# Three projections of five token blocks as seven products of half-size matrices

## The chip, the cores and the metric

The kernel runs on one core of a Trainium2 chip. TensorE (PE) multiplies matrices, with a queue of its own for loading weights (PEld); VectorE (DVE), ScalarE (ACT) and GpSimd (POOL) work on tiles; SyncE (SP) issues almost all DMAs. PE writes to eight PSUM banks of 128 x 512 F32; DVE and ACT read them[...]. The metric is the device time of one execution in microseconds (us), lower is better.

## The reference

The input x has 4 sequences of 1024 tokens with 512 features, so 4096 rows. The first part below is `_L0_attn_ref`, the second `_L0_ffn_ref` (512 to 1536 to 512 features, its weights rounded to fp8), the last two lines join them; their weight arguments are left out:

```python
lam = _decay_lambda(beta)
q = (x @ Wq.T).reshape(Bsz, Ls, NHEAD, HEAD_DIM)
v = (x @ Wv.T).reshape(Bsz, Ls, NHEAD, HEAD_DIM)
ret = _retention_scan(v, lam)              # state = lam * state + v_t
out = (q * ret).reshape(Bsz, Ls, D)
out = _layernorm(out, ln_gamma, ln_beta)
g = jax.nn.silu(x @ Wg.T)
out = out * g
return out @ Wo.T
...
gate = jax.nn.silu(_quantized_matmul(x, gate_w, gate_scale))
up = _quantized_matmul(x, up_w, up_scale)
fuse = gate * up
return _quantized_matmul(fuse, down_w, down_scale)
...
x = x + _layernorm(_L0_attn_ref(_layernorm(x, axis=-1)), axis=-1)
x = x + _layernorm(_L0_ffn_ref(_layernorm(x, axis=-1)), axis=-1)
```

## The kernel before

The 4096 tokens are cut into eight blocks of 512 (NB = 8, TB = 512), the 512 features into four chunks of 128 (NC = 4), the 1536 inner features of the FFN into twelve (NI = 12). One class, `Retention`, does a block's attention half, `Ffn` its FFN half. The main loop runs over the FFN's blocks, t = 0 to 7, and in each over twelve steps i. At a given t three blocks are in work: `a` (block t) is in its FFN, `b` (block t+1) in its attention, `n` (block t+2) is loaded, normalised and transposed, and `l` (block t-1) gets its last layernorm, residual and store.

A step i of the FFN has three parts on PE: `f.gate(i)` and `f.up(i)`, 8 matmuls each in F32R (the activations are kept as an upper part and a remainder, both F32R), and `f.down(i - 2)`, 8 more. Between these parts the loop puts the attention work. For the projections, `project` (line 282) does one chunk of 128 output features for 512 tokens: 4 F32 matmuls of 128 x 512 that add up in one PSUM bank. `v(c)` and `q(c)` run in steps 11 (c = 0, block n), 0, 1 and 2; `scan(c)` runs the recurrence on DVE straight from PSUM, and `y_of(c)` multiplies q by it. Step 3 has chunk 0 of g and the mean over features (`mean`: a matmul of the sum over chunks, split by `halves` into an upper part on ACT and a remainder on DVE, with a matrix of 1/512); `center_y` subtracts it on DVE, squares on ACT and adds the squares on POOL. Step 4 has chunk 1 of g, `var` and `rstd_y` (a root on ACT and a reciprocal on DVE), steps 5 and 6 the rest of g and `z(c)`, which scales and gates chunk c of y. Steps 7 to 10 have the output projection `o(s)` for four groups of 128 tokens, and the moments and sums that follow it; step 11 ends with the transposes of the fourth group.

Order: every engine runs its instructions in the order in which the program issues them (class `InOrder`); the order in the loop is written out by hand. A wait of one instruction therefore holds everything behind it on its engine. The same holds for SP: a DMA that waits for its data keeps the later DMAs back.

PSUM: `ps_a` has two banks that v, q, g, mean, var and o use in turn (name "pa"), `ps_f` two for gate and up (the transposes of step 11 use one of them too), `ps_d` four for the sums of `down`. `halves` and the squares share one scratch tag of two tiles ("ret"), x1n, the FFN's results d and other tiles of 128 x 512 one of four ("tok").

The weights wv_sb, wq_sb and wg_sb (1 MB each) stay in SBUF for the whole run. The input of the projections, xnT, lies as [128 features, 16 groups, 4 chunks, 32 tokens], as it comes out of 32 x 32 transposes by DVE and a trip through DRAM (`send_x`, `fetch_x`); `by_chunk` is its view by chunk, whose runs are 32 tokens long.

Normalising on DVE with two scalars per token row (`center_scale`) serves x of blocks 3 to 7 (`norm_x`) and the FFN's results (`norm`). POOL computes 1/sqrt by a power (`rstd_in_place`).

Of the kernel before, what the change touches and what calls it, by code (L numbers as in the profile page):

```python
# [17 lines left out]
P = 128  # L18
# [5 lines left out]
def retention_ffn_sandwich(  # L24
# [36 lines left out]
    dram = ctx.enter_context(tc.tile_pool(name="dram", bufs=2 * NS, space=bass.MemoryType.DRAM))  # L61
    ps_a = ctx.enter_context(tc.tile_pool(name="ps_a", bufs=2, space=bass.MemoryType.PSUM))
    ps_f = ctx.enter_context(tc.tile_pool(name="ps_f", bufs=2, space=bass.MemoryType.PSUM))
# [228 lines left out]

    homes = {"pa": ps_a, "pf": ps_f, "pd0": ps_d, "pd1": ps_d, "pd2": ps_d, "pd3": ps_d}

    def ps_tile(name, home="pa"):
        return homes[home].tile([P, TB], F32, tag=home, name=name)

    def turn(src, name, home="pa"):
        pt = homes[home].tile([P, NC, P], F32, tag=home, name=name)
        for c in range(NC):  # L300
            pe.transpose(pt[:, c, :], src[:, ts(c, P)], ident)
        return pt

    def turn_by_blocks(dst, src, tag, name):
# [10 lines left out]
        sp.dma_start(dst, m)  # L315

    class Retention:


        def __init__(self, t, xt=None):  # L320
            self.t = t
            self.xt = xt or [load_x(t, s, [sp]) for s in range(NS)]
            self.mv = small.tile([P, NS, 2], F32, tag="mv4", name=f"mv4_{t}", bufs=2)
            self.pv, self.pq, self.pg, self.ret, self.g = {}, {}, {}, {}, {}
            self.po, self.mvo, self.x1n, self.ptx, self.kept = {}, {}, {}, {}, {}
            self.center = shift_scale if t < 2 else center_scale


# [58 lines left out]


        def v(self, c, home="pa", tokens=slice(None)):
            if c not in self.pv:  # L390
                self.pv[c] = ps_tile(f"pv_{self.t}_{c}", home)
            project(self.pv[c], wv_sb, c, [self.by_chunk], tokens)
# [49 lines left out]
        def mean(self):  # L442
            self.mu = ps_tile(f"mu_{self.t}")
            self.average(self.mu)
# [14 lines left out]
        def var(self):  # L459
            var = ps_tile(f"var_{self.t}")  # L460
            self.average(var)
            self.sum = work.tile([P, TB], F32, tag="rstd", name=f"rstd_{self.t}", bufs=1)
            act.activation(self.sum, var, AF.Sqrt, bias=eps_sb)
# [17 lines left out]

        def z(self, c):

            y = self.y
            dve.scalar_tensor_tensor(
                y[:, c, :], y[:, c, :], gamma_sb[:, c : c + 1], self.sum, ALU.mult, ALU.mult
            )
            dve.scalar_tensor_tensor(
                y[:, c, :], y[:, c, :], lnb_sb[:, c : c + 1], self.g.pop(c), ALU.add, ALU.mult
            )  # L490

# [57 lines left out]
    class Ffn:  # L549
# [68 lines left out]
        def rstd(self, s=None):  # L618
            if s is None:
                rstd_in_place(self.mv[:, :, 1], NS)  # L620
            else:
                rstd_in_place(self.mv[:, s, 1:2], 1)

        def rstd_by_root(self, s):
# [181 lines left out]
    for t in range(NB):  # L806
        f, n = Ffn(a), None
        for i in range(NI):
            if t > 0 and (t > 1 or i):
# [10 lines left out]
            if l and not b and i == 3:  # L820
                for s in range(NS // 2, NS):
                    l.scale(s)
            if l and b and i == 3:
                l.norm(0)
                l.add(0)
                l.norm(1)
                l.add(1)
            if l and not b and i in (6, 7):
                for s in range(2 * i - 12, 2 * i - 10):
                    l.norm(s)  # L830
                    l.add(s)
            if n and i == 6 and t > 0:
                n.stats(2)
                n.stats(3)
                n.rstd()
            if b and i == 5:
                b.z(0)
# [6 lines left out]
            for _ in range(look[i] // 2 if t == 1 else 0):  # L844
                next(search)

            if b and t == 0 and i < 2:
                b.q(i + 2, tokens=slice(None) if i else later)
                b.y_of(i + 2)
            if b and t > 0 and i < 3:  # L850
                b.v(i + 1)
                b.scan(i + 1)
            if l and b and i == 2:
                l.stats(0)
                l.stats(1)
            if b and i == 3:
                b.halves()
                units()
                if t == 0:
                    rounds(3, now=False)  # L860
                b.g_of(0)
                b.mean()
                b.center_y()
                if t == 0:
                    n.stats(3)
                    n.rstd()
                    n.shift()
            if b and i == 4:
                b.halves()
                if t == 0:  # L870
                    rounds(3, now=False)
                b.g_of(1)
                b.var()
            if b and i == 5:
                b.g_of(2)
                b.z(1)
            if b and i == 6:
                b.g_of(3)
                b.z(2)
                if t == 0:  # L880
                    b.z(3)
# [10 lines left out]
            if b and 7 <= i <= 10:  # L892
                b.o_moments(i - 7)
            units()
            f.up(i)
            f.fuse(i)
            if b and i == 4:
                b.rstd_y()
            if n and i == 11:
                n.v(0)  # L900
                n.scan(0)
                b.turn_x1n(3, "pf")
                b.upper_of(3)
            if t == 0:
                if i < 8 and i != 3:
                    rounds(3, now=False)
                f.rest(i)
                if i < 3:
                    n.stats(i)
            for _ in range((look[i] + 1) // 2 if t == 1 else 0):  # L910
                next(search)

            if l and b and i == 2:
                l.stats(2)
                l.stats(3)
                l.rstd()
            if l and not b and i in (4, 5):
                l.stats(2 * i - 8)
                l.stats(2 * i - 7)
                if i == 5:  # L920
                    l.rstd()
            if l and b and i == 3:
                l.norm(2)
                l.add(2)
                l.norm(3)
                l.add(3)
            if b and t > 0 and i < 3:
                b.q(i + 1)
                b.y_of(i + 1)
            if b and i == 6 and t > 0:  # L930
                b.z(3)
            if n and i == 5 and t > 0:
                n.stats(0)
                n.stats(1)
# [6 lines left out]
            if n and t > 0 and 6 <= i <= 9:  # L941
                n.norm_x(i - 6)
                n.send_x(i - 6)
# [7 lines left out]
            if n and i == 11:  # L951
                n.q(0)
                n.y_of(0)

# [6 lines left out]
            if b and not n and i == 11:  # L961
                b.turn_x1n(3)
                b.upper_of(3)
                b.rest_of(3)
                f.down(NI - 2)
            if b and i == 4 and 0 < t < NB - 2:
                n = Retention(t + 2)
# [75 lines left out]
```

## Time and profile before

| what | value |
|---|---|
| device time, three runs | 1005.61 to 1007.07 us, median 1006.77 |
| profiled execution | 1006.49 us; its span, first to last instruction, 1004.7 us |
| granted TensorE clock | 0.998 of full |
| DMA | 73.79 MB, mean 73 GB/s |
| a block in the steady part (t = 4) | 121.8 us |
| steps 0 to 2 of it, each | 12.33 us |
| steps 3 and 4, each | 9.34 us |
| steps 5 to 10, each | 8.89 us |
| step 11 | 12.78 us |

The costliest groups of instructions (matmul and weight load apart; in the group view the duration of a matmul is a modelled one, longer than the distance to the next, so the distance between starts is what PE pays):

| group | count | busy us |
|---|---|---|
| up, gate, down matmuls (F32R) | 768, 768, 768 | 215.3, 190.3, about 201 |
| v, q, g, o matmuls (F32, two records each) | 280, 272, 256, 256 | 115.0, 115.3, 114.8, 114.5 |
| DVE remainder of fuse | 90 | 79.4 |
| DVE product of gate and up | 96 | 71.7 |
| ACT SiLU of the gate | 96 | 65.9 |
| POOL x + x1n | 32 | 49.1 |

A row of the time view is: start, duration, engine, line, operation, output and inputs, shapes, count, and in brackets the idle time before it and what ended it. All engine calls go through one helper, so nearly every row says L74; one reads by tile names. pv, pq, pg, mu, var and po are the PSUM tiles of v, q, g, mean, variance and output projection.

### The profile page before, as it was taken

The numbers are of one execution on the slowest core, as the hardware profiler recorded it, in microseconds if no ns is written. First come the engines' busy times: TensorE is split into PE (matmuls) and PEld (weight loads), VectorE is DVE, ScalarE is ACT, GpSimd is POOL, SyncE is SP. The second block draws the span as 40 slices with busy tenths as digits, with TensorE's granted clock in tenths as the row PEclk, the third lists the DMA queues.
The fourth block names the chain that finished last, engine by engine and source line by source line (L and its number), as shares of the span: only waits on it lengthen the run. The fifth ranks groups of instructions, "written<-read, shape, count | busy, mean of one in ns | idle before, by whom it ended". The sixth has DMA issues, their size and how long they took to land.

```text
span 1004.7 us, 9838 instructions
## 1 busy us (share of the span) xinstructions
PE 988.9 (98%) x3518; PEld 653.6 (65%) x3518; DVE 633.8 (63%) x949; ACT 330.1 (33%) x494; POOL 234.8 (23%) x282
## 2 busy tenths in 40 slices
PE   8999999999999999999999999999999999999996
PEld 6456756666666666666666666666666656767885
DVE  5996977527766376753767547674576726746445
ACT  3546574434664133111322114211141111412223
POOL 1405112214122140311413114131132302213020
PEclk9999999999999999999999999999999999999999
DMA  9312314400125004350103402052021510004021
GB/s 296 113 63 91 119 43 105 126 1 22 63 84 147 0 33 146 94 126 1 69 26 108 112 1 84 19 134 79 1 84 37 132 63 11 32 24 123 1 84 42
DMA packets 62608, 73.79 MB, mean 73 GB/s; under 512 B 5856, under 2 KB 36320, under 8 KB 62560
## 3 DMA queue, kind: packets, MB, share of 16 engines
q1 hardware_dynamic: 60976, 72.24, 23.8%
q10 hardware_dynamic: 1584, 0.94, 0.4%
q8 instruction: 27, 0.44, 0.2%
q14 instruction: 21, 0.17, 0.1%
HBM read 43.53 MB, written 29.62 MB: 73 GB/s over the span
## 4 chain that ended last, share of the span: by engine, by line
PE 90%; DVE 4%; DMA 2%; ACT 1%; POOL 1%; issue 1%; SPq 0%; DVEq 0%; POOLq 0%
PE pfu L74 16%; PE pfg L74 16%; PE pd L74 16%; PE pv L74 11%; PE pg L74 10%; PE pq L74 10%; PE po L74 9%; DMA xnT<-mx 1%; DVE scr L74 1%; DMA mx<-xn 1%; DVE st L74 1%; POOL x L74 1%; DVE d L74 1%; DVE xn L74 0%; DMA beta_sb<-in_beta 0%
## 5 line engine op out<-in xcount | busy, mean ns | idle before, releaser
L74 PE MATMUL pfu<-x1nT,up_sb 128*128 128x512 f32 x768 | 215.3, 422 | 0.0
L74 PE MATMUL pfg<-x1nT,gate_sb 128*128 128x512 f32 x768 | 190.3, 390 | 0.4 <-DVE x1nT L74 0.4
L74 PE MATMUL pd<-down_sb,fuse 128*128 128x512 f32 x720 | 188.4, 403 | 0.0
L74 PEld LDWEIGHTS pfu<-x1nT,up_sb 128*128 128x128 f32 x768 | 144.5, 188 | 55.3 <-issue 28.2
L74 PEld LDWEIGHTS pfg<-x1nT,gate_sb 128*128 128x128 f32 x768 | 144.0, 188 | 30.6 <-DVE x1nT L74 0.8
L74 PEld LDWEIGHTS pd<-down_sb,fuse 128*128 128x128 f32 x720 | 135.2, 188 | 38.0 <-issue 10.8
L74 ACT CAST fuse<-gate 128x512 fp32r<-128x512 f32 x90 | 55.7, 618 | 269.0 <-DVE gate L74 269.0
L74 ACT ACTIVATE gate<-pfg,gs_sb 128x512 f32<-128x512 f32 x96 | 65.9, 686 | 221.9 <-PE pfg L74 221.8
L74 DVE SCALAR_TENSOR_TENSOR gate<-pfu,us_sb,gate 128x512 f32<-128x512 f32 x96 | 71.7, 747 | 98.6 <-PE pfu L74 98.4
L74 PE MATMUL pv<-xnT,wv_sb 128*128 128x512 f32 (+1 forms) x280 | 115.0, 557 | 4.0 <-ACT xnT L74 2.7
L74 PE MATMUL pq<-xnT,wq_sb 128*128 128x512 f32 (+1 forms) x272 | 115.3, 567 | 0.0
L74 PE MATMUL pg<-xnT,wg_sb 128*128 128x512 f32 x256 | 114.8, 592 | 0.0
L74 PE MATMUL po<-wo_sb,y 128*128 128x512 f32 x256 | 114.5, 592 | 0.0
L74 POOL TENSOR_SCALAR mv<-mv 128x1 f32<-128x1 f32 (+1 forms) x77 | 18.2, 237 | 314.3 <-DVE mv L74 313.7
L74 PEld LDWEIGHTS pv<-xnT,wv_sb 128*128 128x128 f32 x280 | 52.6, 189 | 52.3 <-issue 45.7
L74 DVE TENSOR_TENSOR fuse<-gate,fuse 128x512 fp32r<-128x512 f32 x90 | 79.4, 883 | 9.7 <-ACT fuse L74 9.7
L74 PEld LDWEIGHTS pq<-xnT,wq_sb 128*128 128x128 f32 x272 | 50.8, 190 | 46.8 <-issue 44.5
L74 PEld LDWEIGHTS po<-wo_sb,y 128*128 128x128 f32 x256 | 48.4, 189 | 50.1 <-issue 47.9
L74 PEld LDWEIGHTS pg<-xnT,wg_sb 128*128 128x128 f32 x256 | 48.4, 189 | 50.1 <-issue 47.2
L74 POOL TENSOR_TENSOR x<-x,x1n 128x512 f32<-128x512 f32 x32 | 49.1, 1533 | 44.4 <-DVE x1n L74 35.5
L74 DVE TENSOR_TENSOR_SCAN ret<-lam,pv 128x512 f32<-128x512 f32 x16 | 19.5, 1219 | 55.4 <-PE pv L74 55.4
L74 DVE BATCH_NORM_STATS2 st<-x 128x6 f32<-128x512 f32 x64 | 43.6, 681 | 14.0 <-POOL x L74 11.2
(114 smaller groups left out, 918.3 us busy)
## 6 DMA issues: line engine op xcount, KB each, us to landing
kept<-x SPq DMA_DIRECT2D x32, 256.0 KB, 2.1
x<-kept SPq DMA_DIRECT2D x32, 256.0 KB, 4.1
x<-in_x SPq DMA_DIRECT2D x28, 256.0 KB, 3.8
out<-d SPq DMA_DIRECT2D x27, 256.0 KB, 2.0
xnT<-mx SPq DMA_DIRECT2D x24, 256.0 KB, 4.7
mxs<-xs SPq DMA_DIRECT2D x84, 64.0 KB, 1.8
x1n<-mxs SPq DMA_DIRECT2D x21, 256.0 KB, 2.7
mx<-xn SPq DMA_DIRECT2D x20, 256.0 KB, 2.3
```

The source lines that it names most:

```text
L74: return lambda *args, **kwargs: tc.keep_in_program_order(op(*args, **kwargs))
```

## The change

For blocks 3 to 7 (`FAST = 3`) the three projections are computed by Strassen's scheme. The weight (512 x 512) and the input (512 x 512 tokens) are cut into halves both ways, and seven products of 256 x 256 by 256 x 256 take the place of eight: four matmuls of 128 x 256 for each product. The precision of the matmuls stays F32.

- `weight_sums` forms four sums of weight quarters for each projection on DVE in steps 0 and 1 of t = 1, and stores them in DRAM (twelve tiles of 256 KB). The resident weights are given up after step 6 of t = 1; their space becomes `t_sums` (four sums of input quarters), `w_ring` (four slots for weight operands) and `mids` (four tiles of 128 x 512 for intermediate results).
- `fetch_weights` loads the operand of a later product from DRAM into the ring: each product, once issued, orders the operand of the fourth product after it, into its own slot.
- `input_sums` forms the four input sums on POOL, at step 11.
- `product` issues the matmuls of the next product. Products that have a term in common add up in the same bank of PSUM; in between, DVE adds banks to `mids`. `take` uses a finished quarter of the result: a scan of half length for v, a product with y for q, a SiLU for g.
- The order is moved: at step 11 `input_sums(1, 2)` before up, two products after up, one and `input_sums(3, 4)` before down, one after down; at steps 0, 1 and 2 a product each after gate, up and down; then two at step 3, three at 4, two at 5, one at 6. The mean is now issued at the end of step 3, the variance at the end of step 4; all scaling of y by gamma is in step 5, all gating in step 6.
- The FFN's results d and x of these blocks are normalised by ACT (`norm_shifted`, `norm_x(.., True)`), with shift and scale made on POOL; the last two additions of d move from step 3 to step 4; statistics of x move to the end of step 5.
- The two "pa" banks get names of their own, pa0 and pa1, so that a product can ask for one.

```diff
@@ banks
-    ps_a = ctx.enter_context(tc.tile_pool(name="ps_a", bufs=2, space=bass.MemoryType.PSUM))
+    ps_a = ctx.enter_context(tc.tile_pool(name="ps_a", bufs=1, space=bass.MemoryType.PSUM))
@@ new, before class Retention
+    FAST = 3
+    H = TB // 2
+    order = [("v", j) for j in (1, 6, 2, 7, 4, 5, 3)]
+    order += [("q", j) for j in (1, 6, 2, 7, 4, 5, 3)]
+    order += [("g", j) for j in (1, 2, 6, 7, 4, 5, 3)]
+    banks = {"v": {1: 0, 6: 1, 5: 0}, "q": {1: 1, 6: 0, 5: 1}, "g": {1: 0, 6: 0, 5: 1}}
...
+    def weight_sums():
+        for k, (src, w) in squares.items():
...
+            for j, x, y, op in (
+                (5, a21, a22, ALU.add), (6, 5, a11, ALU.subtract),
+                (7, a11, a21, ALU.subtract), (3, a12, 6, ALU.subtract),
+            ):
+                t = work.tile([P, D], F32, tag="tok", name=f"sum_{k}{j}", bufs=4)
...
+                dve.tensor_tensor(done[j], x, y, op)
...
+                sp.dma_start(operands[k][j], done[j])
+                yield
...
+    def fetch_weights():
+        n = fetched[0]
+        if n < total_products:
+            k, j = order[n % len(order)]
+            sp.dma_start(w_ring[:, n % RING], operands[k][j])
+            fetched[0] += 1
@@ class Retention
+        def input_sums(self, *which):
+            x = self.by_chunk
+            b11, b12, b21, b22 = (
+                x[:, i : i + 2, g : g + TB // Q // 2, :] for i in (0, 2) for g in (0, TB // Q // 2)
+            )
+            ts_ = [t_sums[:, k].rearrange("p c (g j) -> p c g j", j=Q) for k in range(4)]
+            self.right = {1: b11, 2: b21, 3: b22, 5: ts_[0], 6: ts_[1], 7: ts_[2], 4: ts_[3]}
+            ops = {1: (ts_[0], b12, b11), 2: (ts_[1], b22, ts_[0]), 3: (ts_[2], b22, b12), 4: (ts_[3], b21, ts_[1])}
+            for k in which:
+                dst, x, y = ops[k]
+                pool.tensor_tensor(dst, x, y, ALU.subtract)
...
+        def product(self):
+            k, j = order[self.made]
+            n = (self.t - FAST) * len(order) + self.made
+            self.made += 1
+            w = w_ring[:, n % RING]
+            if j in (1, 6, 5):
+                bank = ps_tile(f"p{k}{j}_{self.t}", f"pa{banks[k][j]}").rearrange("p (c f) -> p c f", c=2)
...
+            bank = self.bank_b if j in (6, 7, 4) else self.bank_a
+            for o in range(2):
...
+                for c in range(2):
+                    pe.matmul(
+                        out_, w[:, c, ts(o, P)], self.right[j][:, c],
+                        start=(j in (1, 6, 5) and o == 0 and c == 0), stop=True,
+                        skip_group_check=True,
+                    )
+            fetch_weights()
+            c12, p1, s167 = (mids[:, m] for m in (1, 2, 3))
+            if j == 1:
+                act.copy(p1, bank)
+            elif j == 6:
+                dve.tensor_tensor(c12, bank, p1, ALU.add)
+            elif j == 7:
+                dve.tensor_tensor(s167, bank, p1, ALU.add)
+            elif j == 2:
+                self.take(k, 0, 0, bank)
+            elif j == 4:
+                dve.tensor_tensor(p1, bank, p1, ALU.add)
+                self.take(k, 1, 0, p1)
+            elif j == 5:
+                dve.tensor_tensor(s167, bank, s167, ALU.add)
+                self.take(k, 1, 1, s167)
+            else:
+                dve.tensor_tensor(c12, bank, c12, ALU.add)
+                self.take(k, 0, 1, c12)
@@ main loop
+            if fast and i in (0, 1, 2, 3, 4, 5, 6):
+                b.product()
...
+            if n and n.fast and i == 11:
+                n.input_sums(1, 2)
...
+                if n.fast:
+                    n.products(2)
...
+            if fast and i < 6:
+                b.product()
...
+                if n.fast:
+                    n.product()
+                    n.input_sums(3, 4)
...
+            if fast and i < 3:
+                b.product()
+            if fast and i == 3:
+                b.mean()
+                b.center_y()
+            if fast and i == 4:
+                b.product()
+                b.var()
+                b.rstd_y()
+            if n and n.fast and i == 11:
+                n.product()
...
+            if t == 1 and i == 6:
+                t_sums = wpool.tile([P, 4, 2, H], F32, tag="wv_sb", name="t_sums")
+                w_ring = wpool.tile([P, RING, 2, H], F32, tag="wq_sb", name="w_ring")
+                mids = wpool.tile([P, 4, 2, H], F32, tag="wg_sb", name="mids")
+                for _ in range(RING):
+                    fetch_weights()
```

## The prediction

> **What bounds the kernel now.** I read the busy row first, then the chain of waits, then TensorE's order in time, because a 98% busy PE is only a limit if nothing releases it late.
>
> ```profile
> PE 988.9 (98%) x3518; PEld 653.6 (65%) x3518; DVE 633.8 (63%) x949; ACT 330.1 (33%) x494; POOL 234.8 (23%) x282
> ...
> PE 90%; DVE 4%; DMA 2%; ACT 1%; POOL 1%; issue 1%; SPq 0%; DVEq 0%; POOLq 0%
> ```
>
> The chain is PE. From block 1's FFN on, the gaps between matmul starts show only two stalls (0.8 us each, at 435.8 and 802.0, the first pv of a block waiting for xnT). So a PE microsecond removed is a microsecond gained, as long as the other engines stay ahead. Two pieces of the chain give the prices of what is swapped:
>
> ```profile
> 12.88 5.18 PE pv L74 x24
> ...
> 684.47 3.44 PE pq L74 x8
> ```
>
> The first is F32 matmuls with 256 tokens, the second with 512 (one F32 matmul leaves two records): 5.18/24 = 0.216 us and 3.44/8 = 0.429 us a record. Halving the tokens halves the time; the kernel's start already runs the new shape.
>
> **PE work removed.** q, v and g cost 16 matmuls each per block: 32 x 0.429 = 13.73 us. Seven products of 4 matmuls of 256 tokens: 56 x 0.216 = 12.09. Saved 1.64 a projection, 4.9 a block, **24.6 us** in five blocks. One product is 1.73 us.
>
> [...] The change has 56 loads where there were 32; at 0.19 us each uncovered, 24 more cost 4.6 us a projection and turn the gain into a loss of 2.9. The trace decides: records 0.216 apart with loads of 0.189 us leave no room for load plus matmul in series, so loads are covered. I take 0.216. The margin is 27 ns, so a slower load would show.
>
> **What the other engines receive, per block.** DVE: 15 additions out of PSUM (0.69, row y<-pq,ret) = 10.3 us, less eight center-and-scale operations (4 x 0.95 + 4 x 0.74 = 6.8) that go to ACT. Busy time by stretches gives DVE 75.7 of block 4's 121.8 us; it fits in sum, not everywhere. POOL: four input sums of 128x512, about 1.5 us each (row x<-x,x1n 1.53). ACT: 3 copies, 8 normalisations. SP: 21 fetches of 256 KB, 27.5 MB in all over 73.8. Each fetch is queued behind its product, but the slot's next product is at least 9 us later, as three products and FFN parts lie between; x<-in_x of equal size lands in 3.8 us. Cost nothing; the cover is those 5 us, and an exposed fetch would cost its excess. The stores queued on SP between fetches (out<-d, behind POOL's adds) end before the next fetch is due. The twelve weight sums in block 1's first two steps (12 x 0.7 us of DVE, which was busy 3.4 of 12.3 us there, plus waits for four scratch tiles to be stored) fit: nothing.
>
> Four places are tight. I schedule each from the trace.
>
> **(a) Product v6 at step 11.** It needs the second input sum. POOL's order puts both sums behind the root for the last x1 tile. Block 4's step 11:
>
> ```profile
> 676.87 1.66 POOL L74 TENSOR_TENSOR x<-x,x1n 128x512 f32<-128x512 f32 x1 [0.92 <-DVE x1n L74]
> 680.00 0.19 POOL L74 TENSOR_SCALAR mv<-mv 128x1 f32<-128x1 f32 x1 [1.46 <-DVE mv L74]
> 680.27 0.54 POOL L74 TENSOR_TENSOR mv<-mv,nhalf 128x1 f32<-128x1 f32 x1
> ```
> ```profile
> 680.44 3.59 PE L74 MATMUL pv<-xnT,wv_sb 128*128 128x512 f32 x8
> ```
>
> POOL is free at 680.8. Two dependent sums, 1.5 + 1.4 (1.29 to 1.66 in the trace, the longer ones beside DVE), end at 683.85. PE starts v1 at 680.44 and is done at 682.17. PE waits until about 683.95: **1.8 us**. Behind v6 stand the transposes, v2 and everything else. Bounds: sums at 1.29 give 1.3; the sums read xnT in runs of 32, a form the trace of POOL lacks, so it may be slower. Nothing below zero. A second wait hides beneath it: v2 needs ACT's copy of v1, and ACT's queue holds an upper half of x1nT that waits for its DMA until 683.8 and a fuse cast, so the copy ends at 685.5; v2 is due at 686.1 with v6 late, at 684.3 without. Were the sums free, 1.2 would remain.
>
> **(b) mu at step 3.** Count from gate(0): PE reaches q3's end at 35.4 and mu at 40.8. Steps 2 and 3 fill DVE (four scales, four stats, five additions, four y). Its last stats end about 35.9; then POOL's root (0.19 + 1.02), shift (0.6) and two half-size sums of y (0.75 each) end at 39.7, ACT's cast at 40.4, DVE's low half at 41.2. Stall **0.3**; 0 to 1, because POOL and DVE stretch one another:
>
> ```profile
> 677.31 1.78 DVE L74 TENSOR_TENSOR fuse<-gate,fuse 128x512 fp32r<-128x512 f32 x1
> ```
>
> This is a 0.66 us operation beside POOL's x add.
>
> **(c) g6 at step 4.** Its bank needs the SiLU of g2, queued on ACT behind the fourth square, which waits for POOL's first square sum, now behind two output adds (2 x 1.3). From mu's end: first square 1.6, POOL's sum done 3.9, fourth square 4.5, two SiLUs 5.9; PE arrives after gate, g2, up = 5.4. Stall **0.4**, 0 to 0.8.
>
> **(d) po(0) at step 7.** y's scale and gate now all stand behind the reciprocal:
>
> ```profile
> 620.21 1.28 ACT L74 ACT_TABLE_LOAD   x1
> 621.51 0.69 ACT L74 ACTIVATE rstd<-var,eps_sb 128x512 f32<-128x512 f32 x1
> ```
> ```profile
> 622.55 3.34 DVE L74 RECIPROCAL rstd<-rstd 128x512 f32<-128x512 f32 x1
> ```
>
> PE's next matmul after var started at 619.86, so root and reciprocal cost 2.45 + 3.3 = 5.7 us from there. Then DVE's order before y's first gated chunk: two fuse remainders and three additions (0.6 apart), two fuse products, four scales, three gates (0.67), four stats with their aggregates (0.82): 3.0 + 6.0 + 3.3 = 12.3, and about 0.5 for crossings from other engines. That is 18.5. PE meanwhile does gate, g4, up, g5, down, gate, g3, up, down, gate: 7 x 1.82 + 3 x 1.73 = 17.9. Stall **0.7**, 0 to 2. Before, this slack was larger, since two chunks of y were done during step 5. DVE then recovers in steps 7 to 10.
>
> **Sum.** Stalls of 1.8 + 0.3 + 0.4 + 0.7 = 3.2 a block, five times 16.0; less 1.0, because the two 0.8 us waits for xnT mostly fall beneath (a). 24.6 - 15.0 = 9.6. The profiled execution took 1006.5 (span 1004.7 and 1.8 around it), the runs' median 1006.8, so they agree. Forecast 1006.5 - 9.6 = **997 us**.
>
> **Rivals.**
> - *Clean gain.* Everything is hidden and PE stays the whole chain: 1006.5 - 24.6 = 982. For it: DVE idles 46 us of a block's 122. Against: POOL's row at 680.8 in (a), an order that the change leaves as it was.
> - *Fewer stalls.* (b) to (d) vanish, as they rest on a few tenths, and (a) stays: 982 + 8 = 990. For it: PE's own wait in (a) gives nothing to (b) to (d), but each small stall delays the ones after and loosens them.
> - *Slower.* POOL's sums of the strided xnT take much longer than a contiguous row. Place: v6, twice the excess. Net gain is 1.9 us a block, so it decides from 1.45 + 0.95 = 2.4 us a sum; at 3.0 the stall grows by 3.1 a block and the time is 997 + 15.5 = 1012. For it: no such POOL row in the trace. Against: the same 512 elements per partition, and only few runs.
> - *Ring too late.* Fetches wait on SP behind stores that wait for POOL; an exposed 1 us on 3 of 21 products gives 982 + 15 + 15 = 1012 as well, but each has 5 us of cover, so I give it little.
> - *Not done as said.* The instruction order shows 420 matmuls of 256 for 240 of 512 and unchanged FFN work. Excluded.
>
> **How the numbers follow.** Forecast case (992 to 1001) 0.46; fewer stalls (984 to 992) 0.28; clean gain (below 984) 0.11; the costs just eat the gain 0.05; slower 0.10, of which ring 0.03. This kernel's measurement tells about 0.2% (2 us) from no change. Faster: 0.46 + 0.28 + 0.11 = 0.85; same 0.05; slower 0.10. The range leaves out the tail of the clean gain and the slower cases: 985 to 1004.
>
> **What would show it.** Right: products as records 0.216 us apart; q, v, g of five blocks 24.6 us shorter; PE idle before v6 about 1.8 us, released by POOL's t_sums; shorter idle before mu, g6 (by ACT) and po (by DVE); PE's share of the chain down, POOL and DVE up. Wrong: records of a product above 0.22 us (weight loads exposed); PE released by a DMA into w_ring; v6 not waiting, or POOL's sums far from 1.45 us; DVE arriving late at v4, v5 or q4, which I cost at nothing with 0.1 to 0.9 us to spare.

## The result and the profile after

The changed kernel takes **992.09 us** (median of 4 runs, 991.50 to 992.31) against 1006.92 us before (4 runs, 1005.61 to 1007.75) on the same chip: ratio 0.9853, 95% interval 0.9836 to 0.987. That is 14.8 us faster; the forecast was 997 with 985 to 1004, so the time lies inside the range and 5 us under the point. The profiled execution took 991.89 us with a span of 990.1 us, at a granted TensorE clock of 0.998.

The busy row and the chain of waits of the changed kernel, from its page:

```profile
span 990.1 us, 11037 instructions
...
PE 968.6 (98%) x3878; PEld 722.0 (73%) x3878; DVE 657.1 (66%) x1006; ACT 365.3 (37%) x549; POOL 256.4 (26%) x337
...
PE 86%; DVE 6%; POOL 3%; ACT 2%; issue 1%; DMA 1%; ACTq 0%; DVEq 0%; SPq 0%; POOLq 0%
```

PE is still busy 98% of the span, but the chain stands on it for 86% instead of 90%: DVE and POOL have gained 2 points each. That fits a gain of which a part was given back in waits. The groups of PE instructions, by form (after the count: busy us, mean ns of one, then idle us before them and what ended it), say where:

```profile
L74 PE MATMUL pv<-t_sums,w_ring 128*128 128x256 f32 x160 | 38.3, 382 | 5.6 <-POOL t_sums L74 5.6
L74 PE MATMUL pg<-t_sums,w_ring 128*128 128x256 f32 x160 | 38.1, 380 | 0.0
...
L74 PE MATMUL pv<-xnT,w_ring 128*128 128x256 f32 x120 | 28.5, 380 | 1.3 <-DMA mxs<-xs 1.3
...
L74 PE MATMUL over_all<-total,mean_r 128*128 128x1 f32 x2 | 0.4, 246 | 1.0 <-DVE total L74 1.0
```

A product's record is given 380 ns since a matmul's end is modelled; from start to start the records stand 0.215 to 0.216 us apart, and the loads of their weights lie beneath them, as in these rows of one product:

```profile
345.60 1.71 PEld L74 LDWEIGHTS pq<-xnT,w_ring 128*128 128x128 f32 x8
345.82 1.89 PE L74 MATMUL pq<-xnT,w_ring 128*128 128x256 f32 x8
```

Below, v6 is product 6 of v, g6 product 6 of g, and so on; gate(0) and po(0) are the first gate chunk of a block and the first group of the output projection. Three places carry nearly all the idle time that the kernel before did not have: v6, which waits for POOL's input sums; a v1, which waits for a DMA; and `over_all`, one sum in the whole run.

I compare by **step lengths**, from a step's first gate matmul to the next one's. For t = 3, where the kernel before had no wait:

| step | before | after | what differs |
|---|---|---|---|
| 0, 1, 2 | 12.33 each | 10.69, 10.66, 10.66 | three products for two chunks |
| 3 | 9.34 | 9.71 | two products for one chunk, mu |
| 4 | 9.34 | 11.19 | three products for one chunk, var |
| 5 | 8.89 | 8.92 | two products for one chunk |
| 6 | 8.89 | 7.18 | one product for one chunk |
| 7 to 10 | 8.89 each | 8.90, 8.89, 8.89, 8.89 | nothing |
| 11 | 12.78 | 14.01 | four products for two chunks, v6's wait |

A chunk is a quarter of a projection, one call of `project`. The sum is 3.2 us a block shorter, and 4.1 where the kernel before had its 0.8 us wait for xnT.

**v6, in step 11 of t = 4.** The timeline of POOL and of PE:

```profile
672.61 0.55 POOL L74 TENSOR_TENSOR mv<-mv,nhalf 128x1 f32<-128x1 f32 x1
673.12 1.26 POOL L74 TENSOR_TENSOR t_sums<-xnT 128x512 f32<-128x512 f32 x1
674.46 1.32 POOL L74 TENSOR_TENSOR t_sums<-xnT,t_sums 128x512 f32<-128x512 f32 x1
```
```profile
672.83 1.89 PE L74 MATMUL pv<-xnT,w_ring 128*128 128x256 f32 x8
675.84 1.99 PE L74 MATMUL pv<-t_sums,w_ring 128*128 128x256 f32 x8 [1.12 <-POOL t_sums L74]
```

The order is the one read from the trace of before: root, then two sums, then v6. The second sum ends at 675.78, v6 starts at 675.84. From starts, v6 is late by 675.84 - 672.83 - 1.73 (v1) = 1.28 us, within 0.1 the same at all five places: 6.4 us.

**The v1 of block 3.** One step 11, at t = 1, has a wait of its own at v1: 1.3 us of idle time in the view, 1.5 from starts. ACT's timeline a step earlier shows its root:

```profile
302.46 1.57 ACT L74 ACTIVATE seen<-gate_sb,neg_max 128x1536 fp8e4<-128x1536 f32 x1
...
304.03 0.80 ACT L74 ACTIVATE xn<-x,mv 128x512 f32<-128x512 f32 x1
```

The change moved block 3's normalisation of x to ACT, where in this block a scan of the weights (`seen`) stands in the queue. The fetch of xnT is issued from 307.90 on and its last part lands at 315.25, 0.14 before v1 starts at 315.39. The kernel before issued it at 306.23; its last part landed at 313.65, 0.3 before its v(0) was due. (The view names a store, mxs<-xs, as the releaser of v1; v1 reads xnT.)

**over_all.** The reduction that it needs stands on DVE behind the product's multiplication (y<-pq,y, 347.75 to 348.44; the reduction 348.35, 0.17 us long); PE waits 1.12 us from starts, once:

```profile
348.35 0.17 DVE L74 TENSOR_REDUCE total<-over 128x1 f32<-128x24 f32 x1
348.67 0.35 PE L74 MATMUL over_all<-total,mean_r 128*128 128x1 f32 x2 [0.96 <-DVE total L74]
```

The ledger: span before 1004.7, less 24.6 of PE records, less 1.6 for the two waits of before that are gone, is 978.5. The measured 990.1 is 11.6 more: 6.4 at v6, 1.5 at that v1, 1.1 at `over_all`, 0.6 at mu (5 x 0.12), 0.3 at g6 (5 x 0.06), at most 0.1 in step 7 with po(0), and 1.6 in small pieces whose places stay open.

### The profile page after: what moved, and what is told of

Its sections match the earlier page's. It is cut to its first block, busy times and chain, and to the rows that moved or that the text cites. A ratio compares the mean times of both kernels' runs of the same rounds, so it can differ in the third digit from the quotient of the medians.

```text
span 990.1 us, 11037 instructions
## 1 busy us (share of the span) xinstructions
PE 968.6 (98%) x3878; PEld 722.0 (73%) x3878; DVE 657.1 (66%) x1006; ACT 365.3 (37%) x549; POOL 256.4 (26%) x337
## 4 chain that ended last, share of the span: by engine, by line
PE 86%; DVE 6%; POOL 3%; ACT 2%; issue 1%; DMA 1%; ACTq 0%; DVEq 0%; SPq 0%; POOLq 0%
PE pfu L74 16%; PE pfg L74 16%; PE pd L74 15%; PE pv L74 10%; PE pg L74 10%; PE pq L74 9%; PE po L74 9%; POOL t_sums L74 1%; DVE st L74 1%; DVE fuse L74 1%; POOL mv L74 1%; DVE scr L74 1%; ACT seen L74 1%; POOL x L74 1%; DVE d L74 1%
## 5 line engine op out<-in xcount | busy, mean ns | idle before, releaser
L74 PE MATMUL pfu<-x1nT,up_sb 128*128 128x512 f32 x768 | 212.1, 418 | 0.0
L74 PE MATMUL pfg<-x1nT,gate_sb 128*128 128x512 f32 x768 | 194.3, 395 | 0.4 <-DVE x1nT L74 0.4
L74 DVE TENSOR_TENSOR fuse<-gate,fuse 128x512 fp32r<-128x512 f32 x90 | 75.6, 840 | 9.1 <-ACT fuse L74 9.1
L74 POOL TENSOR_TENSOR ysum<-y 128x256 f32<-128x256 f32 (+1 forms) x13 | 13.5, 1038 | 188.8 <-DVE y L74 161.1
L74 DVE BATCH_NORM_STATS2 st<-x 128x6 f32<-128x512 f32 x64 | 43.6, 681 | 13.7 <-POOL x L74 11.2
L74 DVE TENSOR_TENSOR mids<-pv,mids 128x512 f32<-128x512 f32 x25 | 17.3, 691 | 46.3 <-PE pv L74 43.4
L74 POOL TENSOR_TENSOR mv<-mv,nhalf 128x1 f32<-128x1 f32 (+1 forms) x75 | 45.3, 604 | 6.2
L74 PE MATMUL pv<-xnT,wv_sb 128*128 128x512 f32 (+1 forms) x120 | 42.9, 508 | 1.6 <-ACT xnT L74 1.6
L74 PE MATMUL pv<-t_sums,w_ring 128*128 128x256 f32 x160 | 38.3, 382 | 5.6 <-POOL t_sums L74 5.6
L74 PE MATMUL pq<-xnT,wq_sb 128*128 128x512 f32 (+1 forms) x112 | 43.4, 531 | 0.0
L74 PE MATMUL pg<-xnT,wg_sb 128*128 128x512 f32 x96 | 43.0, 592 | 0.0
```

The lines of the kernel that those rows point to most:

```text
L74: return lambda *args, **kwargs: tc.keep_in_program_order(op(*args, **kwargs))
```

## The experiments

All are edits of the changed kernel and compute all that it does. To be compared with 992.09; the kernel before ran beside each, with medians of 1006.1 to 1007.4. A difference of about a microsecond is no larger than the distance between these medians, so in runs 3, 4, 6 and 10 the step lengths are the evidence and not the times.

**1. PE work between v1 and v6** (down_first).

```
-                    n.products(2)
+                    n.product()
+                    f.down(i - f.lag, [0, 1])
+                    n.product()
...
-                f.down(i - f.lag)
+                f.down(i - f.lag, [2, 3] if n and n.fast and i == 11 else None)
```

> Half of step 11's down work (tokens 0 and 1, 16 records, about 1.7 us) stands between v1 and v6; the other half stays where it was. Theory (v6 waits for POOL's second input sum, 1.28 us a block, and the wait is lost time): 1.7 us of PE work covers it, v2 then finds ACT's copy of v1 done as well (677.7 in block 4, v2 due at about 678.5), so 5 x 1.28 = 6.4 us go: 985 to 987, and the group pv<-t_sums loses its 5.6 us of idle time. Rival 1 (the wait only moves: the turned x1 reaches gate(0) of the next block later by 1.7 us and gate(0) waits, or v2 waits for the copy): 990 to 992, with idle time at pfg<-x1nT or pv<-xnT in its place. Rival 2 (what ends the wait is not the sums but the ring or ACT): v6 still idle.

Measured 987.33 us (986.89 to 987.97), ratio to before 0.9802 [0.979, 0.9815]. Won: 4.8, not 6.4. The mistake was in my count of the filling: two token tiles of the down projection are 2 x 2 matmuls, 0.227 us apart, 0.91 us and not 1.7. With that the trace answers: v6 waits 0.38 us at four places (0.58 at the one where v1 is late), 1.28 - 0.91 = 0.37. Neither v2 nor the next gate(0) waits, so rival 1 falls: the wait is lost time that other PE work fills one for one. Rival 2 this run alone does not exclude, since v6 still starts when it did; it falls with the rows above, where v6 follows the end of the second sum by 0.06, and with the next run.

**2. The sums first on POOL** (sums_first).

```
+            if n and n.fast and i == 11:
+                n.input_sums(1, 2)
             if b and i >= 8:
                 b.x1_moments(i - 8)
...
-            if n and n.fast and i == 11:
-                n.input_sums(1, 2)
```

> The first two input sums stand on POOL ahead of the root for the last x1 tile instead of behind it. Theory of the prediction (beneath v6's wait lies a second one: v2 waits for ACT's copy of v1, which ACT's queue does not give before about 677.7 in block 4): v6 no longer waits, v2 waits about 0.9 us, and only 0.3 to 0.4 us a block is won: 990 to 991. Rival (the sums are the only wait at this place): the whole 1.28 x 5 = 6.4 us goes: 985.5 to 987.

Measured 998.32 us (997.25 to 1002.03), ratio to before 0.992 [0.9905, 0.9936]: **slower by 6 us**, and neither theory had it. Timelines of this run, again step 11 of t = 4: POOL, PE, and DVE with ACT:

```profile
676.39 1.28 POOL L74 TENSOR_TENSOR t_sums<-xnT 128x512 f32<-128x512 f32 x1 [1.38 <-DMA xnT<-mx]
677.75 1.26 POOL L74 TENSOR_TENSOR t_sums<-xnT,t_sums 128x512 f32<-128x512 f32 x1
679.09 0.19 POOL L74 TENSOR_SCALAR mv<-mv 128x1 f32<-128x1 f32 x1
```
```profile
679.06 1.99 PE L74 MATMUL pv<-t_sums,w_ring 128*128 128x256 f32 x8 [0.20 <-POOL t_sums L74]
681.58 0.63 PE L74 MATMUL pt<-ident,x1n 128*128 128x128 f32 x4 [0.53 <-DVE x1n L74]
683.29 1.78 PE L74 MATMUL pv<-xnT,w_ring 128*128 128x256 f32 x7 [1.08 <-ACT mids L74]
```
```profile
679.96 1.48 DVE L74 TENSOR_SCALAR x1n<-x,mv 128x512 f32<-128x512 f32 x1 [3.56 <-POOL mv L74]
...
682.13 0.62 ACT L74 CAST fuse<-gate 128x512 fp32r<-128x512 f32 x1 [1.60 <-DVE gate L74]
682.65 0.58 ACT L74 COPY mids<-pv 128x512 f32<-128x512 f32 x1
```

POOL now stands still for xnT's landing with the root queued behind it. The root comes 2.7 us after DVE's statistics instead of 0.1, DVE's last x1n waits for it, DVE's fuse product waits behind x1n, ACT's cast waits for the fuse product, and the copy of v1 stands behind that cast: v6 gains 0.9 to 1.1 at four of the five places, the transposes lose 0.7 and v2 1.26. The step is 14.9 to 15.2 long instead of 14.0 (17.1 instead of 15.8 at t = 1), 5.6 us in all. A further 1.6 us of the profiled execution (998.41 us) are not of the edit: they lie in step 4 of t = 0, where the granted clock was at half for 3.4 us (last section). Whether a wait of v2 would remain if the sums were free, as the prediction says beneath (a), this run doesn't tell, since the sums were not free.

**3. Block 3's normalisation back on DVE** (norm3_dve).

```
-                n.norm_x(i - 6, n.fast)
+                n.norm_x(i - 6, n.fast and t > 1)
```

(and no shift for that block).

> Block 3's normalisation of x goes back to DVE (center and scale from mean and root, no shift on POOL); all else as in the changed kernel. Theory (in t=1's step 11 v1 waits 1.5 us because block 3's normalisation sits on ACT behind the fp8 search, so that xnT is fetched 1.7 us late): that wait falls to 0.3 or less and the time to about 990.6 (990.2 to 991.0). Rival (xnT is late there from the ring's first four fetches or the other DMA traffic): the wait stays, 992. v6's wait of the same step stays by both.

Measured 990.81 us (990.14 to 991.71). That step 11 goes from 15.77 to 14.82, and v1's wait from 1.50 to 0.55 from starts: the cause holds, for nearly two thirds of the wait. Counted from the block's first gate, the store of the last mx was issued 1.5 us earlier than in the changed kernel, but the fetch of xnT, which waits for it, only 0.9; and v2 now waits 0.43 for ACT's copy of v1.

**4. The overflow sum ahead of the product** (over_early).

```
+            if t == 2 and i == 1:
+                pass_over()
             if fast and i < 3:
                 b.product()
```

> The matmul that sums the overflow flags (once, t=2 step 1) stands ahead of that step's third product instead of behind it, in a bank of the FFN's pool. Theory (it waits 1.1 us since its DVE reduction is queued behind the product's take): the gap goes, 991.0. Rival (its readers on DVE now hold the take or the bank for pfu of step 2): a gap of 0.5 us or more shows at the product or at pfu and nothing is won, 992. Either way a single microsecond in the whole run.

Measured 990.86 us (990.10 to 991.82). (The edit also takes a bank of `ps_f` for `over_all`.) Step 1 of t = 2 falls from 12.18 to 10.89, no gap is left at `over_all`, and step 2 grows by 0.17. As expected.

**5. Sums of y before the root, in step 3** (ysum_first).

```
-            if fast and i == 3:
-                l.stats(3)
-                l.rstd()
-                l.shift()
             f.gate(i)
...
                 b.product()
+            if fast and i == 3:
+                l.stats(3)
+                l.rstd()
+                l.shift()
```

> In step 3 the last statistics of d, the root and the shift stand behind the third q product instead of ahead of the step, so POOL makes the two sums of y first. Theory (mu waits 0.33 us a block for the sums of y, which stand behind root and shift on POOL): steps 3 fall from 9.71 to 9.38 and the time by 5 x 0.33 = 1.7 us to about 990.3. Rival (the root now comes late to ACT's normalisations of d and POOL's adds, and the square sums behind these: g6 in step 4 waits longer): step 4 grows beyond 11.2 and the time stays at 991.5 or more.

Measured 998.95 us (998.13 to 1002.19), ratio 0.9931 [0.992, 0.9943]: the rival came true, and more. Step 3 stays at 9.71, though the sums of y end 0.4 us earlier in it, so POOL's order was not what mu waits for. Step 4 grows from 11.19 to 12.48; PE's row by form names the place:

```profile
L74 PE MATMUL pg<-t_sums,w_ring 128*128 128x256 f32 x160 | 38.3, 382 | 5.2 <-ACT mids L74 5.2
```

In that run's timelines the root reaches ACT's normalisations later, these hold POOL's adds, these the square sums of y, and the SiLU that frees g6's bank stands on ACT behind the last square. What mu does wait for stands in the timelines of the changed kernel, t = 5, POOL and ACT:

```profile
721.14 1.53 POOL L74 TENSOR_TENSOR ysum<-ysum,y 128x256 f32<-128x256 f32 x2
...
722.73 0.59 ACT L74 COPY mids<-pg 128x512 f32<-128x512 f32 x1 [0.25 <-PE pg L74]
723.21 0.62 ACT L74 CAST half<-ysum 128x512 fp32r<-128x512 f32 x1
```

POOL's sums end at 722.67, but ACT's next instruction in order is the copy of g's first product.

**6. ACT's half ahead of that copy** (halves_first): `b.halves()` of step 3 moves ahead of the `b.product()` before it.

> In step 3 ACT's half of the sums of y stands ahead of ACT's copy of g's first product instead of behind it; POOL's order (root, shift, sums of y) stays. Theory formed after the run that moved the root (mu's 0.33 us are set by that copy on ACT, 722.73 to 723.32 in block 5, and no longer by POOL): the cast starts at 722.7, step 3 falls from 9.71 to 9.38 to 9.45 and the time by 1.3 to 1.7 us to 990.4 to 990.8. Rival (POOL's sums set mu): at best 0.05 us a block, 992.

Measured 991.23 us (990.69 to 992.14). Step 3 falls from 9.71 to 9.59 in every block and PE then runs mu without a gap. So the copy was the cause, but the wait was 0.12 us and not 0.33: I had taken the step's length without a wait as 9.38, which leaves out that a step that begins behind a product and ends behind mu is measured from an earlier point of its first matmul (the record behind a product starts 0.19 early and lasts 0.42, then 0.23 as usual).

**7. The eight normalisations on DVE** (norms_dve): `l.norm` and `n.norm_x(i - 6)` in the place of the forms with a shift, and no shift on POOL.

> The eight center-and-scale operations a block, which the change moved to ACT with a shifted mean, are on DVE again (about 6.8 us a block); the products and all else stay. Theory of the prediction (DVE fits in sum but its margins in steps 3 to 7 are tenths of a microsecond: po(0) has 0.15 us to spare): new waits before g6, var or po(0), 1 to 2 us a block, so 997 to 1002. Rival (DVE idles a third of the time and would have held them anyway): 990.8 to 993.

Measured 997.49 us (996.58 to 998.69), ratio 0.9914 [0.9901, 0.9926]. Step 4 is 12.3 instead of 11.2, again at g6 behind ACT's SiLU (4.4 us in all); po(0) does not wait. So moving them to ACT is worth 5.4 us of the 14.8 net; the 1.2 us that step 11 of t = 1 is shorter here (14.55 for 15.77), as in run 3, are counted against it. It moves two kinds at once, normalisations of d in steps 3 and 4 and of x in steps 6 to 9; since the new wait is in step 4, it is probably the former that carry it, but no run moves them apart.

**8. A ring of two slots, and of one** (ring2, ring1): `RING = 2`, `RING = 1`.

> A ring of two slots instead of four: a fetch is issued when its slot's last product is done, so about 5.4 us (gate or up 1.8, the product between 1.7, up or down 1.8) remain to its use, 3.5 us at v2. Theory (fetches land in 2.6 us as a median and are not held up on SP): no wait of more than some tenths, 992 to 994. Rival (the prediction's ring too late: fetches stand behind stores that wait for POOL): waits of PE at w_ring in steps 3 and 4 or 11, 997 or more.

> A ring of one slot: each fetch is issued when the product before its own is done. This measures what an exposed fetch costs. About 1.8 us of PE work cover it in most places, none between v1 and v6, 0.5 at v2, so with 2.6 us of landing and 0.2 to 0.5 of issue each of 16 to 18 products a block waits 1.0 to 1.3, v6 1.5 more than now, v2 2.2: 5 x (20 to 26) over the 992 of the changed kernel, 1090 to 1120. If landing under this load is longer or shorter, the waits tell by how much.

With two slots 995.23 us (994.85 to 996.17): the steps of t = 1 to 7 are as with four, except step 11, which is 0.4 to 0.6 longer where only the transposes lie between v6 and v2, and v2 is released by its weights. That is 2.6 us; the profiled execution (996.17) has 1.6 more at half clock in step 4 of t = 0 (last section). PE's timeline at t = 4:

```profile
681.61 1.97 PE L74 MATMUL pv<-xnT,w_ring 128*128 128x256 f32 x8 [0.24 <-DMA w_ring<-in_wvT]
```

With one slot 1140.7 us (one run). Most products then wait: half of the waits are 1.1 to 1.4 us (at t = 3 v6 3.5, v2 2.2), on top of the 1.8 us of PE work that lies between most products. So a fetch of 256 KB costs 2.9 to 3.2 us from the end of the product before; its landing is 2.6 to 3.0 as a median. The rival of fetches held up on SP falls: at 5.4 us of cover no product is late, and four slots have more. SP does hold back what stands behind a waiting DMA: in the changed kernel a fetch waits 3.3 us there for its product (issued at 683.61), and x<-kept behind it, which waits for no semaphore of its own, follows at 684.03.

**9. One more statistic before y's gates** (stats_twice): `n.stats(2)` twice in step 6.

> One pair of statistics (0.68 and 0.18 us of DVE) is made twice in step 6 of blocks 2 to 5, between the reciprocal and y's gates. Reading of the trace (the DVE chain behind the reciprocal ends 0.15 us before po(0) is due, so the predicted wait was missed by little): po(0) waits 0.86 - 0.15 = 0.7 us in four blocks, 994.5 to 995. Rival (the chain has slack elsewhere, since DVE idles in it): no wait at po, 992.

Measured 994.65 us (994.39 to 994.94). Step 7 goes from 8.90 to 9.68, po(0) waits 0.68 us in four blocks, released by DVE's y. From start to start the second pair takes 0.80 us of DVE, so 0.80 - 0.68 = 0.12 was the margin; beyond it DVE's time in step 6 is PE's.

**10. The root's table load behind var** (load_late).

```
             self.average(var)
+            if self.fast:
+                one = self.sum[:, 0:1]
+                act.activation(one, var[:, 0:1], AF.Silu)
```

> In the changed blocks ACT applies a SiLU to one column of var (overwritten by the root at once) right ahead of the root, so that the root's table load can't start before var is there, as in the kernel before, where the SiLU of g1 stood between. Theory (step (d) of the prediction was wrong in this one term: 1.28 us of table load lie ahead of var now, and the DVE chain and PE's work were summed about right): 1.28 + 0.2 to 0.4 for the column, less 0.17 of margin, so po(0) waits 1.3 to 1.5 us in blocks 3 to 6; in block 7 DVE has no statistics of a next block there (3.3 us) and po does not wait: 4 x 1.4 = 5.6, 997.3 to 998. Rival (the load's place doesn't matter, the chain has other slack): 992 to 993.

Measured 992.40 us (991.90 to 992.74): the rival is right. The load did move, and the reciprocal with it, but little came of it. ACT's and DVE's timelines of t = 5, first the changed kernel, then this run:

```profile
732.69 1.28 ACT L74 ACT_TABLE_LOAD   x1
736.34 0.69 ACT L74 ACTIVATE rstd<-var,eps_sb 128x512 f32<-128x512 f32 x1 [2.37 <-PE var L74]
...
737.07 3.35 DVE L74 RECIPROCAL rstd<-rstd 128x512 f32<-128x512 f32 x1 [0.50 <-ACT rstd L74]
...
741.78 0.75 DVE L74 SCALAR_TENSOR_TENSOR gate<-pfu,us_sb,gate 128x512 f32<-128x512 f32 x1 [0.22 <-PE pfu L74]
743.44 0.69 DVE L74 TENSOR_TENSOR mids<-pg,mids 128x512 f32<-128x512 f32 x1 [0.91 <-PE pg L74]
```
```profile
736.29 1.28 ACT L74 ACT_TABLE_LOAD   x1
737.59 0.69 ACT L74 ACTIVATE rstd<-var,eps_sb 128x512 f32<-128x512 f32 x1
...
738.31 3.35 DVE L74 RECIPROCAL rstd<-rstd 128x512 f32<-128x512 f32 x1 [1.98 <-ACT rstd L74]
...
743.37 0.68 DVE L74 TENSOR_TENSOR mids<-pg,mids 128x512 f32<-128x512 f32 x1
```

In the changed kernel DVE idles 0.22 + 0.91 us behind the reciprocal because PE's products are not there yet. The reciprocal starts 1.24 us later by the rows, 1.48 relative to PE, which is 0.24 ahead in this run. It uses up this idle time and the margin, and step 7 grows by 0.11 to 0.14. The load's place is worth a tenth a block, not 1.4.

**11. Four edits together** (best): the whole down work of step 11 between v1 and v6, and runs 3, 4 and 6.

> Four edits together: the whole of step 11's down work (8 matmuls, 1.8 us) between v1 and v6, the overflow sum ahead of the third product of its step, block 3's normalisation on DVE, ACT's half of the sums of y ahead of its copy. Theory (the waits are separate, each lost by itself): 6.4 for v6, 1.2 and 1.2 for the two single ones, 1.6 for mu from 992.1: 981.7, 981 to 983. Rival (with the waits gone PE reaches the next tight place earlier, at v2, gate(0), g6 or po(0), and waits there): 984 to 988, and the gaps name the place.

Measured **982.56 us** (981.25 to 985.89, 5 runs), ratio to before 0.9759 [0.9738, 0.978]: 24.4 us under the kernel before and 9.5 under the changed one. The theory of separate waits holds within a microsecond. Step 11 is 12.61 (13.09 at t = 1), and the rows that had the idle time:

```profile
L74 PE MATMUL pv<-t_sums,w_ring 128*128 128x256 f32 x160 | 37.8, 379 | 0.0
...
L74 PE MATMUL pv<-xnT,w_ring 128*128 128x256 f32 x120 | 28.4, 380 | 0.2 <-DMA mxs<-xs 0.2
...
L74 PE MATMUL over_all<-total,mean_r 128*128 128x1 f32 x2 | 0.3, 209 | 0.0
```

## Why the prediction was right, and where its steps were not

**PE's saving: right.** Records 0.216 us apart as in the row of before, with weight loads of 0.19 us beneath them. From 256 to 512 tokens a record of before grows by 0.213 us (0.429 - 0.216), so, by an estimate from these two, about 3 ns of a record are load: the 24 further loads a projection lie covered, and the loss that was weighed against the change, for uncovered loads, did not come. The cross-check is run 11: its span is 980.8, and 1004.7 - 24.6 - 1.6 is 978.5, so all but 2.3 us of the saving can be had.

**(a) v6: mechanism and place right, 1.28 for 1.8.** The mis-sized term is POOL's pair of sums, priced at 1.5 + 1.4; they took 1.26 + 1.32, with their runs of 32 elements no slower here than contiguous adds (two d<-d,x from 724.63 on take 2.54 together; the slower rival needed 2.4 each). Run 1 shows that the wait costs what it lasts. The second wait claimed beneath it is seen only once: in run 3's step 11 of t = 1 v2 waits 0.43 us for ACT's copy of v1. At the other places it is neither shown nor excluded: with v6's wait covered, v2 does not wait in runs 1 and 11, but there the filling delays it as well.

**(b) mu: 0.12 for 0.3, and another releaser.** The estimate ran from POOL's root over the sums to ACT's cast. Its listed terms add up to 39.2 for the sums' end, not 39.7, with which there is no stall; the 39.7 comes near the trace all the same (gate(0) at 683.23, sums' end at 722.67). But the cast starts only at 723.21, behind a copy that the estimate had not placed in ACT's queue; run 6 shows the copy to be what PE waits for, run 5 that moving the root does not help. PE itself comes to mu 41.1 after gate(0) and not 40.8, which makes the wait shorter. That POOL and DVE stretch one another is in the trace of before: DVE's fuse product takes 0.63 to 0.69 us where POOL is idle and up to 1.78 beside a POOL add, x<-x,x1n on POOL 1.26 to 1.29 where DVE is idle and up to 1.72 beside DVE.

**(c) g6: 0.06 for 0.4.** The chain is the one described, behind the fourth square and POOL's adds; it was counted 0.6 too long. In t = 5 the fourth square ends 4.2 us and the second SiLU 5.3 us behind mu, instead of 4.5 and 5.9; PE comes at 5.4 as counted. Runs 5 and 7 show how near it is: either pushes it by about 1.2 us a block.

**(d) po(0): no wait for 0.7** (step 7 is at most 0.02 longer). Two terms failed. The root's table load ran at 732.69, ahead of var, since no SiLU stands between half and root any more (in the kernel before it ran at 620.21, behind g's SiLU, and in run 10 at 736.29, behind the added one). And the 0.5 for crossings was not needed: with the load put back (run 10) DVE and PE take from the reciprocal's end (741.66) to po(0) (753.87) 12.2 us, where the sum had 12.3 and the 0.5, and the wait is 0.11 to 0.14; so this term was the larger error. In the changed kernel DVE even waits for PE in the middle of this chain, which a sum of durations can't show. That the place is tight was right (run 9: 0.12 of margin). In (b) to (d) the differences as printed (41.2 - 40.8, 5.9 - 5.4, 18.5 - 17.9) are each a tenth off the stall stated; in the sum this is 0.1 a block.

**Costs of nothing.** The ring: right. The weight sums: right, steps 0 to 2 of t = 1 are 12.33 as without them. The two waits of before that would vanish under (a): they did. The moves to ACT: counted as relief alone, but for block 3 the queue behind `seen` makes v1 wait 1.5 us, of which run 3 takes away 0.95, and `over_all` behind a product's DVE work costs another 1.1 (run 4). Neither was in the sum.

In all: 16.0 us of waits were forecast for (a) to (d), and 7.4 came, 2.6 less at (a) and 6.0 less at (b) to (d); the waits of before gave 1.6 back instead of 1.0. Against these 9.2 us stand 2.6 us at two places that were not in the sum and 1.6 in small pieces. That leaves 5.0, the distance from 997 to 992. So the nearness of the point is in part luck: errors of opposite sign met. What happened is the rival named "fewer stalls", with (a) a little smaller and two single costs added: 992 against its 990.

## What to carry to other kernels

Where a bound engine's work shrinks, price each wait that the removed work had been covering, and look for the one instruction that comes first of a dependent series (v1, v6): a piece of independent work moved between the two returned 9.5 us together with three smaller edits, most of it at v6. An order on a helper engine is changed only after asking what its first instruction itself waits for: in run 2 sums that waited 1.38 us for a DMA put the root behind them on that DMA's time, and the run was 6 us longer. In a chain over several engines, sum from the last instruction that waits for the bound engine, not from the longest one.

## What was not expected of the hardware

With one ring slot PE stood still 3.5 us at v6 (step 11 of t = 3), and the granted clock then fell. The windows of that run (start:end and length in us, busy us of PE, PEld, DVE, ACT and POOL, granted clock, DMA share, GB/s):

```profile
618.90:622.40 3.50, 0.39 (x2) 0.00 (x0) 0.99 (x2) 1.62 (x3) 3.42 (x4) 1.00 0.61 194
622.40:625.80 3.40, 3.16 (x11) 2.61 (x12) 0.28 (x1) 0.00 (x0) 0.39 (x1) 0.68 0.00 0
625.80:628.20 2.40, 0.46 (x3) 0.06 (x1) 1.70 (x3) 0.59 (x1) 0.00 (x0) 0.50 0.34 109
628.20:632.00 3.80, 3.75 (x9) 3.06 (x10) 0.00 (x0) 0.00 (x0) 0.00 (x0) 0.50 0.00 0
632.00:636.00 4.00, 4.00 (x15) 3.04 (x14) 1.39 (x2) 0.00 (x0) 0.00 (x0) 0.76 0.19 70
```

About 1 us after PE had resumed, its records went from 0.216 to 0.427 us apart, and stayed so for some 10 us. The five v6 of this run wait 3.3 to 3.7 us in the view; at four of them such a stretch begins within 1.5 us of v6's start, before or after it, at the fifth (768.7 us) 5 us later, during v2's wait of 2.9. From 489.6 us to the wait at 618.9, with waits of 1.5 us at most, the clock is full (1.00). How long a wait has to be for this is not shown. In all, the clock is at half for 55 us up to 938 us (the run's mean is 0.973), which by my estimate (records twice as far apart, so half of the work of such a stretch is lost) is up to 27 us of the 1140.7 and part of why this run came out above its expectation of 1090 to 1120.

The length of one wait is not the whole of it. In step 4 of t = 0, which no edit touches, PE waits 1.3 to 1.4 us for var in every run. In the profiled executions of runs 2 and 8 (two slots) 3.4 us at half clock follow (131.6 to 135.0 and 132.3 to 135.7 us; mean clock 0.996), and the step takes 13.1 us instead of 11.5; in that of the changed kernel they do not (1.00 from 130 to 139 us; mean 0.998). Why it comes in some executions only stays open.
